# Norm steps beside context attention: which engine normalizes, which one stores the transposes, and in which slot they run

## The chip, the cores and the metric

The kernel runs on one core of a Trainium2 chip. The metric is the device time of one execution in microseconds. The core has five engines that run side by side and meet at semaphores: TensorE (PE in the profile), VectorE (DVE), ScalarE (ACT), GpSimd (POOL) and SyncE (SP), which issues nearly all DMAs.

## The reference

One transformer block over x of shape 2 x 1024 x 256, with a context of 2 x 154 x 192, 16 heads of 64, all in float32:

```python
h = layernorm(x, ln1);  x = attention(h, h,    sa_*) + x
h = layernorm(x, ln2);  x = attention(h, cond, ca_*) + x
h = layernorm(x, ln3);  p = h @ ff_w1 + ff_b1
a, gate = p[..., :1024], p[..., 1024:]
out = (a * gelu(gate)) @ ff_w2 + ff_b2 + x
```

`layernorm` is over the 256 features with gain and shift; `attention` projects queries, keys and values to 1024 columns, takes a softmax of the scaled scores and projects the result back to 256.

## The kernel before, in words

The order of all work is written out by hand in one loop after another (`tc.manual_schedule()`); no planner moves anything. Each engine does its instructions in the order in which the program issues them.

**Stages.** The two batches have eight head pairs each, so there are 16 units (`units`, eight of batch 0, then eight of batch 1). Self-attention comes first, 8 slots a unit (to about 725 us). Context attention follows with 48 slots, three a unit: slot c belongs to unit ui = c // 3 and n = c % 3, where n says which query tiles (3, 3 or 2 of 8) are scored. The gated layer comes last with 64 slots k, eight for each of eight blocks of two token tiles.

**One slot of context attention.** `cross_first(c)` (from L750) puts the scores of slot c into one of two PSUM tiles "s" (`sc`, L760) and takes the negated maxima on VectorE (`neg`, L765). ScalarE then takes the exponents (`p`, L776) with row sums; one slot later VectorE inverts the sums (`rden`, L784) and GpSimd scales (L787); two slots later VectorE transposes 32 x 32 blocks into `pT_ca` (L803), which DMAs regroup (L820). In this text exponents(c) and sc(c) are those of slot c. Beside it the slots carry other work:

- at n = 0, `cross_queries` of the next unit: `pq_ca` on TensorE (L353), copied to `q_ca` by ScalarE (L368);
- at n = 1, `cross_keys` of the next unit: `pk_ca` (L704), copied to `k_ca` by ScalarE (L708); in even units `context_values`, `pv_ca` (L720), copied to `v_ca` by ScalarE (L729, L730); and `cross_weigh`, the weighted sums `poc` (L839) of the unit two back, copied to `o_ca` by VectorE (L852);
- output projections `py_ca` or `py_sa` (`out_piece`, L457), whose results VectorE adds to x (L464).

A function that issues matmuls returns the store that empties its PSUM tile; `run` puts it on a list, `stores` or `adds`, and `flush` issues that list later.

**PSUM tiles.** There are three pools of two: "s" for scores and for the gated layer's `pa`; "mm" (`mm_tile`); "po" (`sum_tile`). At n = 1, `poc` takes both "po" tiles for its first half and both "mm" tiles for its second half, so it has to wait until whatever held them last has been read out.

**A norm beside other work.** `norm_beside(kind, b)` cuts a norm into steps and puts them on the list `side`. For the wide form (`narrow` is false: the third norm, "ff", and batch 1's second, "ca") a step takes two tiles: `stats` (VectorE, L231, L232), `deviation` (GpSimd, L237, L241), `normalize` (off, L247, then two instructions x to `xn`, L258 on GpSimd or L261 on ScalarE), and `turn`: four PE transposes (`ph`, L271) into one PSUM bank. The store of a turn applies gain and shift on the way from the bank to `hT` (L282 on VectorE, L286 on ScalarE): four pieces of 128 x 128 for "ca", two of 128 x 256 for "ff". `run_work(n, n_side, bank, n_sum)` takes at most `n_side` steps from `side`; a step that turns needs a bank, either `bank` or one of the n "mm" tiles, and otherwise stays where it is:

```python
needs_bank, needs, fn = side[0]
if needs_bank and not bank and n <= 0 or not added.issuperset(needs):
    break
```

So the arguments at each call of `run_work` in the slot loop say in which slots turns may run. The same function takes output projections from `outs`.

**Where the norms lie.** Batch 1's second norm runs in slots 6 to 15, batch 0's third norm in slots 36 to 45, batch 1's third norm in the gated layer from k = 8.

**The gated layer.** `gate_slot(k)` does eight matmuls `pa` (L921), the gelu on ScalarE (L927) and u on VectorE (L930). `sum_slot` does the two matmuls `pf` of the oldest u in `gated` (L944). From k = 5 on, up to two are taken a slot, and one u is always left. The first slots still finish context attention: `poc` of the last two units at k = 1 and k = 4, and the last output projections.

The lines of the profile before are in this listing:

Of the kernel before, what the change touches and what calls it, by code (L numbers as in the profile page):

```python
# [18 lines left out]
def tile_transformer_block(ctx: ExitStack, tc: tile.TileContext, a: dict, out: bass.AP):  # L19
# [4 lines left out]
    B, S, D = x.shape  # L24
# [5 lines left out]
    HP = NPAIR // 2  # L30
    NT = S // P
# [20 lines left out]
    TF = 2  # L52
# [42 lines left out]
    for n in names:  # L95
        k = n_of[n]
# [8 lines left out]
    for n in names[:2]:  # L105
        for r0 in range(0, P, HR):
            (nc.scalar if n == names[0] else nc.sync).dma_start(
                out=cols[r0:r0 + HR, row_of[n]:row_of[n] + NH],
# [95 lines left out]

    hT, vs, qk, oT = {}, {}, {}, {}

    spare = {"bank": mm_tile, "out": mm_tile}
    added = set()


# [1 line left out]
    def norm_pieces(kind, b, first=False):  # L212

        ln = {"sa": "ln1", "ca": "ln2", "ff": "ln3"}[kind]
        g0, b0 = row_of[ln + "_g"], row_of[ln + "_b"]
        st = {}  # L220
        nh = NC if kind == "ff" else NH
        order = tile_order(kind)

        def stats(t):
            if t == 0:
                st["hT"] = hT[kind, b] = p2.tile(
                    [P, nh, NC * S // nh], F32, tag="hT", name=f"hT_{ln}_{b}")
            if t % 2 == 0:
                st["mv", t] = small.tile([P, 2, 2], F32, tag="mv", name=f"mv_{ln}_{b}_{t}")
            s6 = small.tile([P, 6], F32, tag="st", name=f"st_{ln}_{b}_{t}")  # L230
            nc.vector.bn_stats(s6, xt[b, order[t] // GT][:, order[t] % GT, :])  # L231
            nc.vector.bn_aggr(st["mv", t // 2 * 2][:, t % 2, :], s6)  # L232

        def deviation(t):
            mv = st["mv", t]
            var = small.tile([P, 2], F32, tag="var", name=f"var_{ln}_{b}_{t}")
            (nc.vector if first else nc.gpsimd).tensor_scalar(  # L237
                var, mv[:, :, 1], EPS, 1.0, op0=ALU.add, op1=ALU.mult
            )
            rstd = small.tile([P, 2], F32, tag="rstd", name=f"rstd_{ln}_{b}_{t}")  # L240
            nc.gpsimd.tensor_tensor(rstd, var, power, ALU.pow)  # L241
            st["rstd", t] = rstd

        def normalize(t):
            rstd = st["rstd", t]
            off = small.tile([P, 2], F32, tag="off", name=f"off_{ln}_{b}_{t}")
            nc.vector.scalar_tensor_tensor(  # L247
                off, st["mv", t][:, :, 0], -1.0, rstd, op0=ALU.mult, op1=ALU.mult
            )
            pool, tag = (one, "xn") if narrow(kind, b) and not first else (pp_, "P")  # L250

            xn = pool.tile([P, nh, 2, D // nh], F32, tag=tag, name=f"xn_{ln}_{b}_{t}")
            st["xn", t] = xn
            for i in range(2):
                xs = xt[b, order[t + i] // GT][:, order[t + i] % GT, :]
                xs, own = xs.rearrange("p (c d) -> p c d", c=nh), xn[:, :, i, :]
                if kind == "ca" and not narrow(kind, b) or first and i == 1:
                    nc.gpsimd.tensor_scalar(  # L258
                        own, xs, rstd[:, i:i + 1], off[:, i:i + 1], op0=ALU.mult, op1=ALU.add)
                else:  # L260
                    nc.scalar.activation(  # L261
                        own, xs, AF.Identity, bias=off[:, i:i + 1], scale=rstd[:, i:i + 1])

        def turn(t):

            n = 2 if first else 1
            bank = mm_tile if first and t == 2 else spare["bank"]
            ph = [bank(f"ph_{ln}_{b}_{t}_{i}") for i in range(n)]
            for i in range(2 * D // P):

                nc.tensor.transpose(  # L271
                    ph[i * n * P // (2 * D)][:, i % (2 * D // P // n) * P:][:, :P],
                    st["xn", t].rearrange("p c i d -> p (c i d)")[:, i * P:(i + 1) * P], ident)

            def store():
                k = NC * 2 * P // nh
                for c in range(nh):
                    own = st["hT"][:, c, t // 2 * k:(t // 2 + 1) * k]
                    turned = ph[c * n // nh][:, c % (nh // n) * k:][:, :k]
                    gain, shift = cols[:, g0 + c:g0 + c + 1], cols[:, b0 + c:b0 + c + 1]  # L280
                    if first and c < nh // 2:
                        nc.vector.tensor_scalar(  # L282
                            own, turned, gain, shift, op0=ALU.mult, op1=ALU.add
                        )
                    else:
                        nc.scalar.activation(own, turned, AF.Identity, bias=shift, scale=gain)  # L286

            return store

        return (  # L290
            [lambda t=t: stats(t) for t in range(NT)],
            *([lambda t=t, f=f: f(t) for t in range(0, NT, 2)] for f in (deviation, normalize, turn)),
        )

# [6 lines left out]
    def narrow(kind, b):  # L301

        return kind == "sa" or kind == "ca" and b < B - 1
# [233 lines left out]
    stores, adds = [], []  # L537
    later = []

    def run(piece):  # L540
        done = piece()
        if done is not None:
            (adds if getattr(done, "adds", False) else stores).append(done)

    def flush(queue):
        for fn in queue:
            fn()
        queue.clear()
# [22 lines left out]
    def out_pieces(kind, b, half, tiles):  # L571
        outs.extend(lambda t=t: out_piece(kind, b, half, t) for t in tiles)
# [117 lines left out]
    CG = [(t, min(TG, NT - t)) for t in range(0, NT, TG)]  # L690
# [9 lines left out]
    def cross_keys(b, pr, bank=mm_tile):  # L700
        k = qk["ca", b, pr, "k"] = p2.tile([P, S], F32, tag="KT", name=f"k_ca{b}_{pr}")
        pk = bank(f"pk_ca{b}_{pr}")
        for c in range(2):
            nc.tensor.matmul(  # L704
                pk[:, :T], lhsT=wsl["ca", pr, "k"][:, c, :],
                rhs=ctxT[:, c, b * TP:b * TP + T], start=(c == 0), stop=(c == 1),
            )
        return lambda: nc.scalar.copy(k[:, :T], pk[:, :T])  # L708
# [160 lines left out]
    def cross_drain(c):  # L869

        n = c - 2
        if 0 <= n < CA:
            cross_turn(n)
# [11 lines left out]
    FF = B * NBL * NF  # L885
    gated, sums = [], {}
# [79 lines left out]
    with tc.manual_schedule():  # L966
# [85 lines left out]
        for c in range(CA):  # L1052
# [14 lines left out]
            ui, n = divmod(c, len(CG))  # L1067
            nxt = units[ui + 1] if ui + 1 < NU else None
# [9 lines left out]
                run(lambda: cross_keys(*nxt))  # L1078
            flush(adds)
            then = cross_first(c)  # L1080
            flush(stores)
            if c == 1:
                turn_groups(SA - 2)
            if n == 1 and ui > 1 and nxt:
                run(lambda: cross_keys(*nxt, sum_tile))
                flush(stores)
            flush(drain)
            flush(lates)
            lates.append(then())
# [5 lines left out]
            if c == 1:  # L1095
                run(lambda: cross_queries(*nxt))
            elif c == 2:
                run(lambda: cross_queries(*units[2], bank=sum_tile))
            elif c == 3:
                run(lambda: self_values(2 * NU - 1, 0))  # L1100
            elif c == 4:
                run(lambda: self_values(2 * NU - 1, 1))
                run(lambda: cross_keys(*nxt, sum_tile))
            elif n == 0 and ui:
                if nxt:
                    run(lambda: cross_queries(*nxt))
                run_work(0, 1, sum_tile)
            elif n == 1:

                run_work(0, 1, n_sum=1)  # L1110
                if ui % 2 == 0:
                    run(lambda: context_values(*units[ui]))
                run_work(1, 0)
                flush(adds)
                flush(stores)
                cross_weigh(c)
            elif n == 2:
                run_work(0, 1, sum_tile)
                if len(outs) > 2:
                    run_work(2, 0)  # L1120
            cross_regroup(c)
            for _ in range(min(2, len(later))):
                later.pop(0)()

        for k in range(FF):
            c = CA + k
            flush(adds)
            gate_slot(k)
            flush(stores)
            flush(lates)  # L1130
            if k == 3 * len(CG) - 1:
                norm_beside("ff", B - 1)
            cross_drain(c)
            cross_weigh(c)
            cross_regroup(c)
            if k == 0:
                out_pieces("ca", B - 1, 0, range(NT - 2 * TF, NT))
            if k == len(CG) + 1:
                out_pieces("ca", B - 1, 1, range(NT))
            if k > len(CG) + 1:  # L1140
                for _ in range(min(2, len(gated) - 1)):
                    run(sum_slot)
                flush(stores)
            run_work(2, 1)
            if later:
                later.pop(0)()
# [35 lines left out]
```

## Time and profile before

| what | value |
|---|---|
| median of 3 runs | 1145.99 us (1143.33 to 1146.7) |
| profiled execution, its own time | 1144.58 us |
| its span, first to last instruction | 1142.8 us |
| mean granted TensorE clock | 0.997 |
| busy: TensorE, VectorE, ScalarE, GpSimd | 1112.5, 835.4, 647.0, 672.7 us |
| context attention, about | 725 to 943 us |
| gated layer, about | 943 to 1140 us |

How to read the profile. A line of a stage table gives the stage, its length, and the busy time of PE, PEld (weight loads), DVE, ACT and POOL with their instruction counts, then the granted TensorE clock, the DMA share and GB/s. A line of the waits gives who waited for whom, the sum in microseconds, how many times, and the longest. A line of a timeline gives start, length, engine, source line, operation, output and inputs, shapes, count, and in brackets the idle time of the engine before it and what ended it. A line of the instructions of one source line gives the shortest, median and longest duration in ns, and the first and last start in us. A timeline's lengths overlap a little for pipelined matmuls, so the distance between two starts is what a piece takes.

### The profile page before, as it was taken

The page shows a single profiled execution, that of the slowest core. Times are in us where ns is not written, and L with a number is a line of the kernel's source. Part 1 is how long each engine was busy: PE and PEld are TensorE (multiplying, and loading weights), DVE is VectorE, ACT ScalarE, POOL GpSimd, SP SyncE. Part 2 cuts the span into 40 slices and gives each one's busy share as a digit, 9 for nine tenths or more (in the row PEclk, how much of TensorE's full clock was granted, in tenths as well). Part 3 has the DMA queues.
Part 4 walks back from the last instruction along what each step waited for, and adds up shares of the span by engine and source line. Part 5 has one row for each costly group of instructions (what it writes and reads, how often), then busy time and mean ns, then how long its engine had stood idle before and what let it go on. Part 6 is the DMA issues. An engine that isn't in the chain of part 4 may idle for free.

```text
span 1142.8 us, 36749 instructions
## 1 busy us (share of the span) xinstructions
PE 1112.5 (97%) x14372; PEld 688.5 (60%) x14372; DVE 835.4 (73%) x1183; ACT 647.0 (57%) x2082; POOL 672.7 (59%) x1568
## 2 busy tenths in 40 slices
PE   8999999999999999999999999998999989999998
PEld 5444444545545545545545554675777667888887
DVE  4888898898898999899988989766666754322222
ACT  4666666666765665666666666657555661041111
POOL 2777777878777777777777777756544542020000
PEclk9999999999999999999999999999999999999999
DMA  3212122201111111111111010256655523000000
GB/s 84 63 50 49 37 49 52 53 18 40 35 28 40 31 31 45 31 31 40 31 31 40 22 31 15 56 148 175 162 130 127 124 52 70 10 10 10 19 10 19
DMA packets 104910, 59.94 MB, mean 52 GB/s; under 512 B 32090, under 2 KB 95522, under 8 KB 104738
## 3 DMA queue, kind: packets, MB, share of 16 engines
q1 hardware_dynamic: 103506, 56.93, 20.9%
q8 instruction: 114, 1.87, 0.7%
q10 hardware_dynamic: 1232, 0.66, 0.2%
q14 instruction: 58, 0.48, 0.1%
HBM read 27.91 MB, written 2.10 MB: 26 GB/s over the span
## 4 chain that ended last, share of the span: by engine, by line
PE 85%; ACT 5%; DVE 3%; DMA 2%; POOL 2%; SPq 1%; issue 1%; DVEq 0%; POOLq 0%; ACTq 0%
PE po L526 18%; PE s L479 18%; PE pa L921 10%; PE py_sa L457 5%; PE py_ca L457 5%; PE pf L944 5%; PE pk_sa L353 4%; PE pq_sa L353 4%; PE pv_sa L384 4%; PE poc L839 4%; PE pq_ca L353 3%; ACT p L490 2%; PE sc L760 2%; SPq L500 1%; DVE st L641 1%
## 5 line engine op out<-in xcount | busy, mean ns | idle before, releaser
L490 ACT ACTIVATE p<-s,st 128x512 f32<-128x512 f32 x512 | 344.8, 686 | 204.9 <-DVE st L641 198.2
L591 POOL TENSOR_SCALAR p<-p,rd,ee 128x512 f32<-128x512 f32 x512 | 385.6, 767 | 45.6 <-DVE rd L587 44.3
L641 DVE TENSOR_REDUCE st<-s 128x2 f32<-128x1024 f32 x256 | 301.2, 1217 | 34.5 <-PE s L479 18.5
L605 DVE STREAM_TRANSPOSE pT<-p 128x1024 f32<-128x1024 f32 x256 | 302.2, 1217 | 0.3 <-POOL p L591 0.3
L479 PE MATMUL s<-k_sa,q_sa 64*32 64x512 f32 x4096 | 253.1, 596 | 13.0 <-ACT p L490 12.4
L526 PE MATMUL po<-pT,v_sa 64*64 64x256 f32 x4096 | 236.6, 380 | 0.8 <-DVE pT L605 0.8
L526 PEld LDWEIGHTS po<-pT,v_sa 64*64 64x64 f32 x4096 | 150.7, 133 | 110.7 <-issue 33.4
L787 POOL TENSOR_SCALAR p<-p,rden 128x154 f32<-128x154 f32 x256 | 96.8, 398 | 95.4 <-DVE rden L784 94.9
L479 PEld LDWEIGHTS s<-k_sa,q_sa 64*32 64x32 f32 x4096 | 65.9, 106 | 135.9 <-issue 66.0
L776 ACT ACTIVATE p<-sc,neg 128x154 f32<-128x154 f32 x256 | 96.6, 415 | 79.9 <-DVE rden L784 78.5
L930 DVE SCALAR_TENSOR_TENSOR u<-pa,cols,gate 128x256 f32<-128x256 f32 x64 | 31.0, 484 | 123.1 <-ACT gate L927 123.1
L921 PE MATMUL pa<-hT_ln,wf 128*128 128x256 f32 x512 | 120.7, 379 | 0.0
L927 ACT ACTIVATE gate<-pa,cols 128x256 f32<-128x256 f32 x64 | 30.3, 473 | 148.8 <-PE pa L921 148.7
L921 PEld LDWEIGHTS pa<-hT_ln,wf 128*128 128x128 f32 x512 | 96.9, 190 | 13.1 <-issue 0.2
L490 ACT ACTIVATION_READ_ACCUMULATOR p<-s,st 128x1 f32 x512 | 103.8, 203 | 0.0
L384 PEld LDWEIGHTS pv_sa<-sa_wv,hT_ln 64*128 64x128 f32 x1024 | 59.1, 188 | 17.4 <-DMA st<-st 7.5
L944 PE MATMUL pf<-wf,u 128*128 128x256 f32 x256 | 65.1, 379 | 0.2 <-DVE u L930 0.2
L514 POOL TENSOR_TENSOR zz<-ee,st 128x8 f32<-128x8 f32 x128 | 25.9, 202 | 66.4 <-ACT ee L512 66.4
L457 PE MATMUL py_ca<-ca_wo,o_ca 128*128 128x256 f32 x256 | 60.7, 388 | 4.3 <-ACT hT_ln L286 3.2
L384 PE MATMUL pv_sa<-sa_wv,hT_ln 64*128 64x128 f32 x1024 | 63.0, 276 | 0.6 <-ACT v_sa L393 0.6
L765 DVE TENSOR_REDUCE neg<-sc 128x6 f32<-128x924 f32 (+1 forms) x48 | 48.0, 1002 | 17.5 <-PE sc L760 17.4
L457 PE MATMUL py_sa<-sa_wo,o_sa 128*128 128x256 f32 x256 | 59.5, 385 | 0.0
(87 smaller groups left out, 1248.5 us busy)
## 6 DMA issues: line engine op xcount, KB each, us to landing
wf<-pT_ca SPq DMA_DIRECT2D x128, 128.0 KB, 2.5
st<-st SPq DMA_DIRECT2D x512, 1.0 KB, 1.8
v_sa<-v_sa SPq DMA_DIRECT2D x32, 256.0 KB, 3.4
sa_wq<-in_L_xattn_sa_wq_dram SPq DMA_DIRECT2D x32, 128.0 KB, 2.9
sa_wk<-in_L_xattn_sa_wk_dram SPq DMA_DIRECT2D x32, 128.0 KB, 2.9
sa_wv<-in_L_xattn_sa_wv_dram SPq DMA_DIRECT2D x32, 128.0 KB, 2.9
ca_wq<-in_L_xattn_ca_wq_dram SPq DMA_DIRECT2D x32, 128.0 KB, 3.0
wf<-in_L_xattn_ff_w_dram SPq DMA_DIRECT2D x12, 256.0 KB, 3.8
```

The costliest lines, as they stand in the source:

```text
L353: nc.tensor.matmul(pq[r][f:f + m, at:at + n], lhsT=wt[own, c, f:f + m], rhs=h[own, c, t0:t0 + n], start=(c == 0), stop=(c == NH - 1), tile ...
L384: nc.tensor.matmul(pv[r][:, i * P:(i + 1) * P], lhsT=h[own, c, i * P:(i + 1) * P], rhs=wt[own, c, :], start=(c == 0), stop=(c == NH - 1), ...
L457: nc.tensor.matmul(py[:, :D], lhsT=o[:, i, t * P:(t + 1) * P], rhs=wo[kind][:, half * HP + i, :], start=(i == 0), stop=(i == HP - 1),)
L479: nc.tensor.matmul(sc[a4 * KB:(a4 + 1) * KB, j, :], lhsT=q[r, c:c + KB], rhs=k[r, h * HB:(h + 1) * HB], start=True, stop=True, tile_positi ...
L490: nc.scalar.activation(pr[:, j, :], sc[:, j, :], AF.Exp, bias=st[:, 0, 0, i, j:j + 1], accum_out=st[:, 0, 1, i, j:j + 1],)
L526: nc.tensor.matmul(po[a2][j * DH:(j + 1) * DH, :QH // 2], lhsT=v[r, t, e, j * DH:(j + 1) * DH], rhs=pT[r, j * NK + n, :], start=(t == 0 an ...
L591: nc.gpsimd.tensor_scalar(pr[:, j, :], pr[:, j, :], rd[:, c:c + 1], ee[:, 0, c:c + 1], op0=ALU.mult, op1=ALU.mult,)
L605: nc.vector.transpose(halves[h][:, :, c:c + KB], groups.pop(0).rearrange("p j (n k) -> p (j n) k", k=KB))
L641: nc.vector.tensor_reduce(st[:, 0, 0, i, :], sc[i], AX.X, ALU.max, negate=True)
L787: nc.gpsimd.tensor_scalar(pr_[:, j, i, :T], pr_[:, j, i, :T], rden[:, j, i:i + 1], 1.0, op0=ALU.mult, op1=ALU.mult,)
L921: nc.tensor.matmul(pa[:, half, :TF * P], lhsT=w1[:, c, half * DF + f * P:half * DF + (f + 1) * P], rhs=h[:, c, t0 * P:(t0 + TF) * P], star ...
L944: nc.tensor.matmul(sums[blk][i][:, :D], lhsT=sums[blk, "u"][:, f, i * P:(i + 1) * P], rhs=w2[:, f, :], start=(f == 0), stop=(f == NF - 1),)
```

## The change

It is one diff with seven parts.

1. `normalize`: the condition for GpSimd no longer asks for "ca", so every wide norm is normalized by GpSimd; before, the third norm was normalized by ScalarE (16 instructions of 128 x 256).
2. A flag `spare["turned"]`: from slot 7 to the end of context attention it is set, and the stores of turns go to VectorE (16 pieces of 128 x 128 and 4 of 128 x 256); at the start of the gated layer it is cleared.
3. At n = 1, `cross_keys` is issued before the stores are flushed, and its copy is put at the head of the list, ahead of the query copies.
4. Turning steps may run at n = 1 with a "po" tile, their store issued at once, ahead of the output projections and `poc`; no longer at n = 0, and at n = 2 only in unit 3. So the turns of batch 1's second norm move from slots 11, 12, 14 and 15 to 11, 13, 16 and 19, and those of batch 0's third norm from 41, 42, 44 and 45 to 43, 46 and, in the gated layer, k = 0 and k = 1.
5. At the start of the gated layer, the list of output projections is filled before the drain, two projections run ahead of `poc` at k = 1, and the last eight projections are made available at k = 5 rather than k = 4, so after the `poc` of k = 4 the next `pa` follows.
6. Batch 1's third norm begins one slot later, at k = 9.
7. In the last two slots two u instead of one are left in `gated`.

```diff
-                if kind == "ca" and not narrow(kind, b) or first and i == 1:
+                if not narrow(kind, b) or first and i == 1:
                     nc.gpsimd.tensor_scalar(
...
-                    if first and c < nh // 2:
+                    if spare["turned"] or first and c < nh // 2:
                         nc.vector.tensor_scalar(
...
             then = cross_first(c)
+            if n == 1 and ui > 1 and nxt:
+                run(lambda: cross_keys(*nxt, sum_tile))
+                stores.insert(0, stores.pop())
             flush(stores)
             if c == 1:
                 turn_groups(SA - 2)
-            if n == 1 and ui > 1 and nxt:
-                run(lambda: cross_keys(*nxt, sum_tile))
-                flush(stores)
...
                 if nxt:
                     run(lambda: cross_queries(*nxt))
+                run_work(0, 1)
+            elif n == 1:
+
+                spare["turned"] = True
                 run_work(0, 1, sum_tile)
-            elif n == 1:
-
-                run_work(0, 1, n_sum=1)
+                flush(stores)
+                run_work(0, 0, n_sum=1)
                 if ui % 2 == 0:
                     run(lambda: context_values(*units[ui]))
                 run_work(1, 0)
...
             elif n == 2:
-                run_work(0, 1, sum_tile)
+                run_work(0, 1, sum_tile if ui == HP - 1 else None)
...
+        spare["turned"] = False
         for k in range(FF):
...
-            if k == 3 * len(CG) - 1:
+            if k == 3 * len(CG):
                 norm_beside("ff", B - 1)
+            if k == 0:
+                out_pieces("ca", B - 1, 0, range(NT - 2 * TF, NT))
+            if k == 1:
+                run_work(2, 0)
+                flush(adds)
             cross_drain(c)
             cross_weigh(c)
             cross_regroup(c)
-            if k == 0:
-                out_pieces("ca", B - 1, 0, range(NT - 2 * TF, NT))
-            if k == len(CG) + 1:
+            if k == len(CG) + 2:
                 out_pieces("ca", B - 1, 1, range(NT))
             if k > len(CG) + 1:
-                for _ in range(min(2, len(gated) - 1)):
+
+                for _ in range(min(2, len(gated) - (1 if k < FF - 2 else 2))):
                     run(sum_slot)
```

More of the change, by code (lines that the diff above doesn't have):

```diff
@@ L205, in tile_transformer_block @@
     hT, vs, qk, oT = {}, {}, {}, {}
-    spare = {"bank": mm_tile, "out": mm_tile}
+    spare = {"bank": mm_tile, "out": mm_tile, "turned": False}
     added = set()
```

## The prediction

> **What bounds the kernel now.** I read the page's first part, then the stage table, then TensorE's waits, then the timelines of the stalled stretches. TensorE is busy nearly all the time, so only its idle time can be won:
>
> ```profile
> PE 1112.5 (97%) x14372; PEld 688.5 (60%) x14372; DVE 835.4 (73%) x1183; ACT 647.0 (57%) x2082; POOL 672.7 (59%) x1568
> 770.00:802.00 32.00, 29.13 (x296) 19.02 (x295) 20.75 (x47) 21.02 (x90) 20.68 (x54) 1.00 0.69 172
> 802.00:909.00 107.00, 107.00 (x936) 76.82 (x938) 71.43 (x158) 64.11 (x294) 57.13 (x164) 1.00 0.56 131
> 909.00:931.00 22.00, 18.77 (x149) 12.88 (x141) 11.01 (x27) 12.16 (x46) 8.06 (x23) 0.92 0.29 62
> ```
>
> The second column is TensorE. The stage table shows where context attention leaves it idle: at 770 to 802, where batch 1's second norm runs beside it (slots 11 to 16 of 48), and after 909, where batch 0's third norm does (slots 41 to 45). Between them nothing is idle. The waits of TensorE in 770 to 966 are six rows:
>
> ```profile
> PE py_ca L457 <- ACT hT_ln L286: 3.2, 1, 3.2
> PE ph_ln L271 <- ACT xn_ln L261: 1.7, 2, 1.5
> PE poc L839 <- ACT hT_ln L286: 1.3, 1, 1.3
> PE poc L839 <- ACT v_ca L730: 1.0, 1, 1.0
> PE py_ca L457 <- DVE o_ca L852: 1.0, 2, 0.5
> PE ph_ln L271 <- POOL xn_ln L258: 0.6, 1, 0.6
> ```
>
> Together 8.8 us, four of the six rows due to ScalarE or its norm work. TensorE's timeline of the longest, and ScalarE's beside it:
>
> ```profile
> 916.67 0.79 PE L704 MATMUL pk_ca<-ctxT,ca_wk 96*128 96x154 f32 x4
> 920.68 3.44 PE L457 MATMUL py_ca<-ca_wo,o_ca 128*128 128x256 f32 x8 [3.23 <-ACT hT_ln L286]
> 923.97 1.89 PE L720 MATMUL pv_ca<-ca_wv,ctxT 96*128 96x256 f32 x8
> ```
>
> ```profile
> 917.64 1.11 ACT L261 ACTIVATE xn_ln<-x,off_ln,rstd_ln 128x256 f32<-128x256 f32 x2
> 918.62 1.10 ACT L368 ACTIVATE q_ca<-pq_ca 128x512 f32<-128x512 f32 x2
> 919.58 1.05 ACT L286 ACTIVATE hT_ln<-ph_ln,cols 128x256 f32<-128x256 f32 x2
> ```
>
> ScalarE runs six exponents, a normalization, two query copies, and only then the store that frees the PSUM bank for py_ca. That row also costs twice: its eight matmuls hold TensorE from 920.68 to 923.97, 3.29 us, where eight usually take 1.73 (the later py_ca in this slot).
>
> [...] after 3.23 us idle the granted clock of the stage is 0.92, and 3.29 - 1.73 = 1.56 us go. [...] six of these twelve ran at 770 to 802 beside a VectorE busy 20.75 of 32 us, and none takes over 557 ns:
>
> ```profile
> L258 POOL TENSOR_SCALAR xn_ln<-x,rstd_ln,off_ln x12: 547/549/557, 6.8 to 792.8; 128x256 f32<-128x256 f32 x12
> L282 DVE TENSOR_SCALAR hT_ln<-ph_ln,cols x8: 399/402/410, 8.2 to 15.1; 128x128 f32<-128x128 f32 x8
> ```
>
> **The change part by part.** TensorE's 14372 matmuls stay the same; only their order moves, and SP's list of DMAs is unchanged. I lay the new order on the old durations from start to start: ph .59 us, pk .63, sc .73 to .99, pq 3.53, py and pv 1.73, poc 2.75.
>
> (1) *Slots 41 to 43.* The two ph of slots 41 and 42 go; one comes after pk of slot 43. xn is on GpSimd (2 x .55 = 1.1 us) and issued slots earlier. ScalarE then does exponents(42) by about 915.7, the k copy when pk ends (916.3, +.35), q copies to 917.7. py_ca takes k's bank at 916.8: no wait. VectorE's queue in slot 43 is neg 1.1, rden .2, turns .9, four statistics 1.1, off .3, then the store; two pieces of 128x256, which I price at .42 to .48 each by L852 and L930 (no such store is in the trace): done at 920.0. poc needs that bank at 921.8. Slack 1.8. Gain: the hole (917.39 to 920.68) 3.29 + cold clock 1.56 + a ph that leaves .58 = **5.4**.
>
> (2) *Slots 44 to 47.* Without the ph between them, sc(44), sc(45), sc(46) follow each other, and sc(46) needs the score bank of sc(44), free when exponents(44) end. Before, that was 931.06 to 933.59, 2.53 us after sc(44) ended; so sc(46) waits 1.67. This takes the place of the 1.56 that the late xn cost; queued behind it on TensorE are ph, two py and poc. Then ph, py, py, and poc needs VectorE's store and py's add, behind neg 1.1, rden, turns .9: about .65 more. Row by row: before 12.22 us, after 11.86. Gain **.4**, where a ph that goes later is already .58.
>
> (3) *Start of the gated layer.* The two deferred ph come here, +1.2; ScalarE stores them behind the gates (py of k=1 needs that bank: free 19.6 us after sc(44) starts, needed at 19.7, so no room). Of the two .51 waits for o_ca, each .58 with its restart, the first stays, now in front of ph; the second goes, as pa follows poc where py did. Net **-.4** (loss).
>
> (4) *Slots 12 to 19 of batch 1's norm.* Slot 13: ph follows pk, hole .63 gone, but pv waits .5 for a query copy that is now behind the k copy. The next two poc banks wait for VectorE's four stores, 4 x .33 = 1.35 (two start .33 apart: 0.73 for the pair), behind neg, rden, turns, off: 1.05. The v_ca wait (really 1.67 from start to start) goes, ScalarE having shed 1.5 us of stores. Gain .7. Slot 16: poc is wanted 7.45 us after sc(14) starts, the store ends at 10.0, wait 2.55 against 1.44 + .16 now, with one ph less: loss .4. Slot 19 takes a ph without a wait: loss .6. Net **-.2**. Here the unknown is large: each store's end is a sum of six VectorE steps; bounds -2 and +1.5. Behind each store on VectorE stand the v_ca memset, the adds of py and the o_ca copies; who waits is poc.
>
> (5) *k copy before the query copies, 13 units.* In unit 10 (slot 31), pk ends 834.63; k is done at 835.0, the first query at 835.5; pv wants its bank at 836.20. Cover .7; taken at nothing. If gone, .34 a unit, 4.4 us.
>
> (6) *Last sums.* One pf pair moves behind the last pa, so the last u is covered: the .22 us hole goes. Gain **.2**.
>
> (7) *Batch 1's third norm*, one slot later, on GpSimd: 8 x .55 = 4.4 us in slots of 2.6 us where GpSimd is nearly free; TensorE does not wait there now and hT is not needed until k = 32. ff_b adds slip from slots 46 to 48 to after k = 1 (8 x .73 = 5.8 us, needed near k = 11). Nothing; if that cover failed, .5 to 1 us. GpSimd's eight xn beside attention fall into its idle gaps (4.4 us at 911).
>
> Sum: 5.4 + .4 - .4 - .2 + .2 = **5.4 us** off the profiled execution's 1144.58 (span 1142.8): 1139.2. The runs' median, 1145.99, is 1.4 above that execution; less 5.4 it gives 1140.6. I take 1140.0.
>
> **Rivals.**
> - *Given back* (chance .2): the bank of ph is now released at the end of VectorE's queue, and slots 13, 16 and 46 trade a ScalarE wait for a VectorE one about 1 us longer each than I reckon, and k=1 shows 1 us. Speaks for it: VectorE is already the busiest after TensorE (73%), and in slot 16 I find a longer wait myself. Against: slot 43 keeps 1.8 us of slack. Gain 5.4 - 4 = 1.4: 1144.
> - *Slower* (.09): ScalarE's queue now stops at the k copy until pk is done, the query copies behind it, and TensorE's next bank with them, in all 13 units. It decides when the first query copy comes over .7 us later than reckoned; at 1.4 us late each unit loses .7, 9.1 us in all, less 5.4: 3.7 slower, about 1149. Against it: exponents end before pk in units 9 to 13 anyway, so the copy waits only some .2 us.
> - *Larger gain* (.09): the stores are not last, slots 13 and 16 lose nothing: their 3.6 us of waits come back, 1136.5.
> - *My forecast* (.62): 1138 to 1142.5.
>
> **How the numbers follow.** About 0.3%, 3.4 us, is what a measurement of this kernel can tell from no change; faster by that means below 1142.55. The forecast lies under it almost wholly (.61), the larger gain wholly (.09), the first rival in a sixth (.03): faster .73. Within: .01 + .16, .17 with rounding. Slower: .09 and .01 of the first rival: .10. Range: 1136 to 1145, which leaves out the slow rival and part of the large gain.
>
> **What would show it.** Right: in slot 43 no py_ca wait on hT_ln, and a granted clock of 1.0 there; sc waiting some 1.7 us on exponents in slot 46; poc waiting on VectorE in slots 13 and 16; the last pf without a gap; one o_ca wait left. Wrong: py_ca or pv_ca waiting on query copies in unit after unit; a wait above 3 us with slow matmuls behind it; TensorE's idle sum in 770 to 966 not falling by 4 us.

## The result, and the profile after

The changed kernel takes 1138.26 us (median of 7 runs, 1136.75 to 1140.36) against 1144.66 us for the kernel before on the same chip (7 runs, 1142.03 to 1146.7): ratio 0.9946, 95% interval 0.9929 to 0.9962, which is 4.4 to 8.1 us. Predicted were 1140.0 us and a gain of 5.4 us. The profiled execution took 1138.26 us, its span 1136.5 us against 1142.8.

The first part of the page, then the table of stages after (both read as before: the second column of the table is TensorE, the eighth the granted clock):

```profile
PE 1109.5 (98%) x14372; PEld 689.9 (61%) x14372; DVE 841.2 (74%) x1203; ACT 632.0 (56%) x2046; POOL 681.2 (60%) x1584
```

```profile
770.00:802.00 32.00, 29.40 (x288) 19.19 (x282) 26.37 (x63) 17.69 (x83) 22.06 (x59) 1.00 0.77 190
802.00:909.00 107.00, 106.93 (x957) 77.05 (x955) 71.32 (x160) 61.59 (x284) 55.68 (x159) 1.00 0.55 129
909.00:931.00 22.00, 20.20 (x155) 15.07 (x152) 17.49 (x41) 14.61 (x70) 13.96 (x40) 0.92 0.42 92
```

ScalarE lost 15.0 us of work; GpSimd gained 8.5 and VectorE 5.8. TensorE's matmuls are the same 14372. The last row still has a clock of 0.92. The stall of slot 43 has gone, but in its place there is another piece at half clock, which is to say a stretch in which the granted TensorE clock is 0.5. TensorE's waits from 770 to 966, all the rows:

```profile
PE poc L839 <- DVE hT_ln L282: 1.9, 2, 1.7
PE sc L760 <- ACT p L776: 1.8, 1, 1.8
PE py_ca L457 <- DVE x L464: 0.8, 1, 0.8
PE ph_ln L271 <- DVE o_ca L852: 0.6, 1, 0.6
PE pv_ca L720 <- ACT q_ca L368: 0.5, 1, 0.5
```

8.8 us of waits have become 5.6, and the 3.2 us wait of py_ca on hT_ln is not among them. TensorE's timeline shows slot 43 without a hole; before, the same py_ca came 3.23 us late:

```profile
913.24 0.79 PE L704 MATMUL pk_ca<-ctxT,ca_wk 96*128 96x154 f32 x4
913.87 0.60 PE L271 MATMUL ph_ln<-ident,xn_ln 128*128 128x128 f32 x4
914.41 1.99 PE L457 MATMUL py_ca<-ca_wo,o_ca 128*128 128x256 f32 x8
916.24 1.89 PE L720 MATMUL pv_ca<-ca_wv,ctxT 96*128 96x256 f32 x8
```

Slots 45 and 46 of the same execution:

```profile
925.92 1.06 PE L760 MATMUL sc<-k_ca,q_ca 64*128 64x154 f32 x12 [1.80 <-ACT p L776]
926.90 0.98 PE L271 MATMUL ph_ln<-ident,xn_ln 128*128 128x128 f32 x4
927.67 5.02 PE L457 MATMUL py_ca<-ca_wo,o_ca 128*128 128x256 f32 x16
```

The predicted wait of sc on the exponents is there (1.80 us). The sixteen py_ca behind it take 5.02 us, where sixteen take 3.62 elsewhere. The granted clock is 0.5 from 927.1 to 930.5 us, and nothing in the prediction had that.

**Where the time went.** From here on the traces are compared in stretches, from the first score matmul of one slot to that of another ("k = 9": the first `pa` of that slot). The last column is what the prediction's sum gives for the stretch, minus for a gain.

| stretch | before | after | difference | predicted |
|---|---|---|---|---|
| start to slot 12 | 774.58 | 773.15 | -1.43 | 0 |
| slot 12 to 14 | 13.49 | 12.51 | -.98 | -.7 |
| slot 14 to 17 | 12.28 | 12.01 | -.27 | +.4 |
| slot 17 to 21 | 15.74 | 16.36 | +.62 | +.6 |
| slot 21 to 41 | 93.27 | 93.48 | +.21 | 0 |
| slot 41 to 44 | 20.91 | 15.03 | -5.88 | -5.4 |
| slot 44 to 47 | 12.22 | 12.84 | +.62 | -.4 |
| slot 47 to k = 9 | 51.06 | 52.45 | +1.39 | +.4 |
| k = 9 to the end | 149.21 | 148.65 | -.56 | -.2 |

The first row is no part of the change: from slot 7 to slot 12 both take 27.4 us, up to slot 7 the order is the same, and over the thirteen profiled kernels of this study the row runs from 772.1 to 776.1. Part of that scatter is the clock: before has a piece at half clock there, from 94.2 to 97.6 us, and after has none. The work around it takes 22.0 us in before and 19.9 to 20.6 in the ten traces without such a piece, which by itself is as much as the row's difference. Without the row the profiled difference is 4.85 us. The slow py_ca of slot 46 cost 1.43 us and do not come with every execution of the changed kernel (experiment 6); without that too it is 6.28 us.

### The profile page after: what moved, and what is told of

Read it like the earlier page. It is cut to its first block, busy times and chain, and to the rows that moved or that the text cites. A ratio compares the mean times of both kernels' runs of the same rounds, so it can differ in the third digit from the quotient of the medians.

```text
span 1136.5 us, 36749 instructions
## 1 busy us (share of the span) xinstructions
PE 1109.5 (98%) x14372; PEld 689.9 (61%) x14372; DVE 841.2 (74%) x1203; ACT 632.0 (56%) x2046; POOL 681.2 (60%) x1584
## 4 chain that ended last, share of the span: by engine, by line
PE 79%; ACT 6%; DVE 4%; DMA 4%; POOL 3%; SPq 2%; issue 2%; DVEq 0%; POOLq 0%; ACTq 0%
PE po L526 16%; PE s L479 16%; PE pa L921 9%; PE py_sa L457 5%; PE pf L944 5%; PE py_ca L457 5%; ACT p L490 4%; PE pk_sa L353 4%; PE pq_ca L353 4%; PE pv_sa L384 4%; PE poc L839 4%; PE pq_sa L353 3%; PE sc L760 2%; SPq L500 2%; DVE st L641 2%; DMA st<-st 2%
```

## The experiments

All runs are against the kernel before on the same chip; its medians were 1145.31, 1144.99 and 1145.19 us in the three groups. "After" is the changed kernel. A stretch that no edit touches comes out the same within .2 us from run to run, unless a piece of it runs at half clock; only start to slot 12 and slot 17 to 21 scatter.

**1. GpSimd's normalization alone**, in the kernel before:

```diff
-                if kind == "ca" and not narrow(kind, b) or first and i == 1:
+                if not narrow(kind, b) or first and i == 1:
```

> The kernel before with one edit: the third norm is normalized by GpSimd; stores, slots and copies stay. Theory (order of ScalarE's queue): in slot 43 the py_ca wait shrinks only by the two normalizations that stood ahead of the store, 3.2 to about 2.1 us, and the wait of ph for xn in slot 45 (1.7 us) turns into a short wait of sc for exponents; 2 to 4 us faster than before, the larger end if the clock stays up after the shorter wait. Rival (ScalarE's load alone was the cause): the py_ca wait is gone and nearly the whole gain of the change is there, 5 to 6 us.

Measured: 1143.27 us, ratio 0.9975 (0.9965 to 0.9985). Slots 41 to 44 take 17.63 us, 3.28 less than before, but slots 44 to 47 take 14.72, 2.50 more. Its waits:

```profile
PE ph_ln L271 <- POOL xn_ln L258: 3.2, 3, 2.4
PE py_ca L457 <- ACT hT_ln L286: 0.9, 1, 0.9
```

Of the 3.2 us wait of py_ca .9 are left, since ScalarE still stores the turn. And in the old slots GpSimd's xn comes too late for its turn: ph waits 2.4 us in slot 45, with half clock behind it from 930.8 to 934.2 us. Of the 2.50 us about .9 is the longer wait (2.4 us in place of 1.5) and the rest the clock. So neither expectation was quite right: the whole gain, about 2 us, is at the low end of the theory's, but the py_ca wait shrank further than to 2.1 us, and what the normalization gains in one slot it gives back in good part two slots on.

**2. The stores back on ScalarE**, the rest as after:

```diff
-                spare["turned"] = True
                 run_work(0, 1, sum_tile)
```

> The changed kernel with the stores of turns left on ScalarE (the flag is never set); GpSimd normalization and new slots stay. Theory (the store's engine decides, because in the new slots ScalarE's store stands behind the six exponents of its slot): poc waits about 2.5 us in slot 13, 3.5 to 5 us in slot 16 with a half-speed clock behind it, about 1.4 us in slot 46; 4 to 7 us slower than the changed kernel, so near the kernel before. Rival (only the slots count): the same time as the changed kernel within 1 us.

Measured: 1144.4 us, ratio 0.9992 (0.9985 to 0.9999). Slot 43 is as good as after (15.03 us from 41 to 44). What is lost is lost in slots 12 to 14 (13.83 us, +1.32) and 14 to 17 (16.80, +4.79), and .8 us in slot 46, if after's slow piece there is left out:

```profile
PE poc L839 <- ACT hT_ln L286: 5.9, 3, 4.0
```

```profile
794.96 0.65 PE L839 MATMUL poc<-wf,v_ca 64*64 64x256 f32 x4
799.56 1.54 PE L839 MATMUL poc<-wf,v_ca 64*64 64x256 f32 x10 [3.95 <-ACT hT_ln L286]
```

Once the turn stands right ahead of poc, its store on ScalarE lies behind six exponents, and poc waits 3.95 us in slot 16 against 1.73 with VectorE. The rest of the 4.79 us, some 2.6, is half clock from 798.0 to 804.8 us. The theory holds. So the stores on VectorE are the price at which the later turn is to be had; in slot 43 itself they are worth nothing.

**3. The turns in their old slots**, normalization and stores as after:

```diff
-                run_work(0, 1)
+                run_work(0, 1, sum_tile)
             elif n == 1:
                 spare["turned"] = True
-                run_work(0, 1, sum_tile)
-                flush(stores)
-                run_work(0, 0, n_sum=1)
+                run_work(0, 1, n_sum=1)
...
-                run_work(0, 1, sum_tile if ui == HP - 1 else None)
+                run_work(0, 1, sum_tile)
```

> The changed kernel with turns back in their old slots (11, 12, 14, 15; 41, 42, 44, 45), stores on VectorE and all normalizations on GpSimd. Theory (the bank's release decides, not the slot): slot 43 waits at most 1 us, ph again stands between the scores of slots 44 to 46 so their wait for exponents is mostly filled and the clock stays up; equal to the changed kernel or 1 to 3 us faster. Rival (the new slots carry the gain): the py_ca wait in slot 43 is back near 3 us, 4 to 5 us slower than the changed kernel.

Measured: 1141.41 us, ratio 0.9956 (0.9943 to 0.997). Slots 41 to 47 take 31.86 us in place of 27.87, and 47 to k = 9 49.89 in place of 52.45, as two turns fewer are left for it. Summed from slot 12 it is 1.96 us worse than after. Its largest wait is GpSimd's xn again (3.4 us, longest 2.4), not the store. Both expectations missed: the old slots are slower, but by 2 us in the traces and not by 4 to 5, and slot 43 has no py_ca wait over .4 us. Both traces have one piece at half clock in slots 44 to 47, so it does not make the difference.

**4. The normalization back on ScalarE**, turns and stores as after (the condition of experiment 1, reversed).

> The changed kernel with the third norm's normalization back on ScalarE (16 instructions of 128x256), the rest as changed. Theory (once the turns are moved to slots 43, 46, k = 0 and k = 1, ScalarE has gaps of 3.8 and 5.0 us where these instructions fall, so the engine matters little): 1138.5 to 1139.5, slots 41 to 44 15.0 to 15.6 us. Rival (GpSimd's normalization is itself what the gain in slot 43 comes from): slots 41 to 44 above 17 us with a py_ca wait on ScalarE, and over 1140.5. The normalization on GpSimd with the old slots gained 3.3 us there, of 5.9, so that run leaves both open.

Measured: 1137.46 us, ratio 0.995 (0.9933 to 0.9967). Slots 41 to 44 15.03 us, as after; 44 to 47 11.41; only 47 to k = 9 is .33 longer. Slots 14 to 17, whose program is that of after, took 13.69 in place of 12.01; the 1.68 us are half clock (below). The rival falls: with the turns moved, GpSimd's normalization is worth some .4 us.

**5. The k copy behind the query copies again:**

```diff
                 run(lambda: cross_keys(*nxt, sum_tile))
-                stores.insert(0, stores.pop())
```

> The changed kernel with one line out: the copy of k_ca is flushed in its old place, behind the query copies. My theory (part 5 of the prediction: the copy order is worth nothing either way, because .7 us cover the query copies): 1138.3 us, within 0.7 of the changed kernel; only in slot 13 does the .55 us wait of pv_ca on the query copy go, and in slot 43 pk_ca's bank comes .55 us a copy later, which costs under 1 us. Rival 1 (the k copy ahead delays the query copies in unit after unit): the stretch from slot 21 to slot 41, 93.48 us in the changed kernel, becomes shorter by over 1 us. Rival 2 (the k copy ahead is what the new order of slot 43 lives on, since py_ca takes k's bank): slots 41 to 44 grow from 15.03 us by 1.1 us or more, with a wait of py_ca on k_ca, and the run is near 1140.

Measured: 1138.65 us, ratio 0.9955 (0.9943 to 0.9967). Slots 21 to 41 93.31 us against 93.48: the copies' order costs the quiet units at most .17 us in all. Slots 41 to 44 take 15.65 us, .62 more:

```profile
PE py_ca L457 <- ACT k_ca L708: 1.2, 2, 0.6
```

So the rival that the prediction priced at 9 us is wrong, and "nothing" is nearly right: where a turn and a py_ca follow pk, the copy ahead saves .6 us. Of rival 2 the mechanism is right and its 1.1 us too much. (Slots 14 to 17 took 13.70 us here, with poc at half clock behind waits of .6 and 1.1 us.)

**6. The last sums as before, in the changed kernel; and 7. the last sums alone, in the kernel before** (there the lines of the diff change places):

```diff
-                for _ in range(min(2, len(gated) - (1 if k < FF - 2 else 2))):
+                for _ in range(min(2, len(gated) - 1)):
```

> The changed kernel with the end of the gated layer as before: one u is left in the last slots, not two. My theory (part 6): only the last u is uncovered again, a .2 us gap ahead of the last pf, so from k = 9 to the end 148.9 us in place of 148.65, and about 1138.5. Rival (the measured .5 us of that stretch all come from here): 149.15 us. Second rival (the stretch's gain comes from batch 1's third norm, one slot later and on GpSimd, not from the sums): 148.65, no change.

> The kernel before with part 7 of the change alone: two u are left in the last two slots. Theory (the .5 us from k = 9 to the end is this part, since undoing it in the changed kernel gave all of it back): 149.21 - .5 = 148.7 us from k = 9 to the end, 1144.5 us in all. Rival (it needs the later third norm as well): 149.2. The run also shows a second time the context slots of the kernel before. If the half clock after a wait of 3.23 us in slot 43 follows from the wait, slots 41 to 44 take 20.9 us again with eight py_ca in 3.3 us; if it is chance there too, as after the 1.7 to 1.8 us waits (slow in two of the executions, fast in three others of the same program part), they may take 19.3.

Measured: experiment 6 149.14 us from k = 9 to the end (+.49), experiment 7 148.72 (-.49). So this part is worth .49 us with either kernel, as the first rival had it and not the .2 of my theory, and the third norm on GpSimd one slot later at most .07. The end of the kernel before shows the gap:

```profile
1137.10 1.03 PE L944 MATMUL pf<-wf,u 128*128 128x256 f32 x4
1138.35 1.13 PE L944 MATMUL pf<-wf,u 128*128 128x256 f32 x4 [0.22 <-DVE u L930]
```

The times of whole runs can't show so little: 1138.7 us, ratio 0.9948 (0.9933 to 0.9962), and 1145.79 us, ratio 1.0004 (0.9996 to 1.0013).

Both executions bear on the slow py_ca too. Experiment 6 has the same wait in slot 46, word for word, and then sixteen matmuls at full clock:

```profile
926.25 1.06 PE L760 MATMUL sc<-k_ca,q_ca 64*128 64x154 f32 x12 [1.80 <-ACT p L776]
927.24 0.66 PE L271 MATMUL ph_ln<-ident,xn_ln 128*128 128x128 f32 x4
927.73 3.62 PE L457 MATMUL py_ca<-ca_wo,o_ca 128*128 128x256 f32 x16
```

It takes 11.41 us from slot 44 to 47 where after took 12.84. Experiment 4 shows the reverse in slot 16, where after had no slow matmul behind the same wait:

```profile
795.79 0.86 PE L839 MATMUL poc<-wf,v_ca 64*64 64x256 f32 x10 [1.72 <-DVE hT_ln L282]
...
797.13 1.90 PE L839 MATMUL poc<-wf,v_ca 64*64 64x256 f32 x12
```

The second twelve take 1.02 us in the execution of after. Over the profiled executions with the same program there: after the 1.8 us wait of slot 46 one of five has half clock (after; not experiments 2, 4, 5, 6), after the 1.72 us wait of slot 16 one of seven (experiment 4). In slot 45 of the old order, after 1.50 + .16 us, one of two: 44 to 47 takes 13.81 us in experiment 7 and 12.22 in the kernel before. After the 3.23 us wait of slot 43 both profiled executions have it (20.91 and 21.14 us), and so has the one after 3.95 us (experiment 2). But even the 3.23 us wait is not followed by half clock every time: of the 72 executions of the kernel before in the three groups, five, all on one chip, have a mean granted clock of 1.000, and a single piece of 3.41 us at half clock would bring it to 0.9985. The last section lays out where such pieces begin.

**8. Work put into slot 45.** The sc of slot 46 waits 1.80 us for exponents; output projections are at hand to fill it. Two in one kernel, one in the next:

```diff
                 run_work(0, 1)
+                if ui == NU - 1:
+                    run_work(2, 0)      # the second kernel: run_work(1, 0)
```

> The changed kernel with the two output projections of slot 46 issued in slot 45, between the scores of slots 45 and 46. Theory (sc of slot 46 waits for the exponents of slot 44 because nothing stands between, and the pause is what halves the clock behind it): the wait of 1.8 us and the 1.4 us of slow py_ca go, 2.5 to 3.2 us faster than the changed kernel. Rival (the wait moves to poc of slot 46, which needs VectorE's store): the same time within 1 us, with a poc wait of about 2 us.

> The changed kernel with one output projection (eight matmuls, 1.73 us) taken in slot 45, ahead of the scores of slot 46, which there wait 1.80 us for the exponents of slot 44. With two projections the wait went but the weighted sums of slot 46 then stood 1.98 us behind VectorE's store. Theory A (VectorE's queue, max of slot 46 first and then the store, sets the end, and each projection ahead of the scores delays both equally): the score wait falls to about .1, the py_ca that ran at half clock after it is fast again, no wait over .5 us comes in its place, and slots 44 to 47 and the start of the gated layer together gain about 1.8 + 1.4 = 3.2 us less the .4 us that a new wait may take: from slot 44 to k = 9 some 62.3 us in place of 65.29. Theory B (whatever is filled in ahead comes back as a wait of poc on the store): 65 us, no gain. The wait and the slow clock are separate: if the wait goes and the slow matmuls stay, the clock was not lowered by the wait.

Measured: with two 1139.32 us, ratio 0.9937 (0.9923 to 0.995), slots 44 to 47 13.59 us with poc at half clock; with one 1136.06 us, ratio 0.9932 (0.9908 to 0.9955), 11.41 us. The wait of sc is gone in both, and poc waits in its place, 1.98 and 1.58 us. The profile names no releaser ("issue"), but VectorE's timeline beside it does, with one projection. TensorE's resumes at 930.38:

```profile
930.38 1.15 PE L839 MATMUL poc<-wf,v_ca 64*64 64x256 f32 x14 [1.58 <-issue]
```

```profile
927.29 1.10 DVE L765 TENSOR_REDUCE neg<-sc 128x6 f32<-128x924 f32 x1
928.31 0.18 DVE L784 RECIPROCAL rden<-den 128x6 f32<-128x6 f32 x1
928.41 0.86 DVE L803 STREAM_TRANSPOSE pT_ca<-p 128x320 f32<-128x320 f32 x2
929.20 0.17 DVE L247 SCALAR_TENSOR_TENSOR off_ln<-mv_ln,rstd_ln 128x2 f32<-128x2 f32 x1
929.29 0.98 DVE L282 TENSOR_SCALAR hT_ln<-ph_ln,cols 128x256 f32<-128x256 f32 x2
```

The store ends at 930.27, the poc follows. Theory B's mechanism holds: from slot 44 to 47 it is 11.41 us with and without the projection (experiment 6), where the clock held. From slot 44 to k = 9 that makes 63.86 us, after's 65.29 less its 1.43 us of half clock. Slot 46's store stands behind the reciprocal of slot 45's sums. In this execution VectorE has no idle time from 922.1 to 930.6 us, and slot 45's exponents end at 928.28, .03 us before the reciprocal starts, so its own queue and ScalarE hold the store about equally; in experiment 6, without the projection, the reciprocal waits .25 us for the exponents. The median is 2.2 us under after's all the same. All five executions of the kernel with one projection have a mean clock of 1.000, of after two of seven; how much of the 2.2 us that explains stays open.

**9. The first projection of k = 1 into a "po" tile**, with one projection in slot 45:

```diff
             if k == 1:
-                run_work(2, 0)
+                run_work(0, 0, n_sum=1)
+                run_work(1, 0)
                 flush(adds)
```

> The changed kernel with one projection in slot 45, ahead of the scores of slot 46, and at k = 1 the first of the two projections put into a 'po' tile. With the first edit alone slots 44 to 47 took 11.41 us, as without it where the clock held; the wait moved from sc to poc. Theory: py_ca at k = 1 waits .81 us for the 'mm' tile whose add stands on VectorE behind a transposition, while both 'po' tiles are free, so the wait goes and k = 47 to k = 9 takes 51.65 us in place of 52.45; slots 44 to 47 stay at 11.4; near 1135.5. Rival (the add of the 'po' projection then comes late for poc, which takes both 'po' tiles first): 52.4 us, with a poc wait of some .8 us at k = 1.

In after, the add on VectorE and the py_ca that waits for it:

```profile
942.33 0.41 DVE L464 TENSOR_TENSOR x<-py_ca,x 128x256 f32<-128x256 f32 x1
942.80 3.72 PE L457 MATMUL py_ca<-ca_wo,o_ca 128*128 128x256 f32 x16 [0.81 <-DVE x L464]
```

Measured: 1137.54 us, ratio 0.9933 (0.9921 to 0.9945); 47 to k = 9 51.37 us in place of 52.45. The .81 us wait of py_ca on x is gone, with 1.08 us, so the theory holds for the stretch. The expected 1135.5 us were missed: the ratio is that of the projection alone (0.9932), and start to slot 12 was 2.9 us longer in this profile than in that one.

**10. That, without the turn in slot 46:**

```diff
-                run_work(0, 1, sum_tile)
+                run_work(0, 1, sum_tile if ui < NU - 1 else None)
                 flush(stores)
```

> The last kernel without the turn in slot 46: batch 0's third norm turns in slot 43 and at k = 0, 1 and 2. In slot 46 the store of the turn stands on VectorE behind the reciprocal, which waits for the exponents of slot 45, so poc waits 1.58 us for its bank. Theory (the store is what poc waits for; what is left is the adds of the projections in the same queue): slots 44 to 47 take 10.0 to 10.6 us in place of 11.41, of which .5 us is the turn itself that comes back at k = 2; a net gain of .3 to .9 us over the kernel with the turn. Rival (the adds, behind the same reciprocal, release poc hardly sooner): 10.9 us, which is only the turn, and no net gain.

Measured: 1135.46 us, ratio 0.9914 (0.99 to 0.9928), the fastest kernel here, about 9.7 us under the kernel before. Slots 44 to 47 take 10.39 us, 1.02 less; 47 to k = 9 takes 51.81, .44 more for the turn. Net .58, as the theory had it. Against after, the stretches from slot 44 to k = 9 give 62.20 in place of 65.29 us, or 63.86 without the slow py_ca.

```profile
PE poc L839 <- DVE x L464: 0.7, 1, 0.7
PE ph_ln L271 <- DVE o_ca L852: 0.6, 1, 0.6
```

What is left in slot 46 is the add of a projection, in the same queue of VectorE.

## Why the prediction was right, and where its steps were off

The mechanism, the place and nearly the size were right. Point by point, with the half clock of slot 46, which does not come every time, taken out:

- **(1) Slots 41 to 43: 5.88 us, predicted 5.4.** The wait and the half clock went, as reckoned. Of the .5 us above the forecast .3 are in the scores: without a ph between them, sc of slots 41 and 42 and pq take 4.85 us in place of 5.15. The step counts the 1.56 us of half clock as certain, which it is not. The five executions of the kernel before at a mean clock of 1.000 have a median of 1140.99 us, the two of after 1137.19 and 1137.56. By these few the change is worth some 3.6 us where the clock stays up on both sides (the forecast without its half clock is 3.8), and half clock, which the kernel before meets more often, is at least a part of the rest of the 6.4 us (the mean of the 72 clocks is 0.9965, of after's seven 0.998, which is one such piece more in each execution). What the step did not say is which part carries it. Experiments 1 and 4 tell: the normalization alone gains 3.28 us there and gives 2.50 back, in part through the clock; with the later turn ScalarE's normalization does as well.
- **(2) Slots 44 to 47: .81 us gained (11.41), predicted .4.** The term mis-sized is poc's ".65 more" for VectorE's store: in experiment 6, with no slow py_ca, there is no such wait. The sc wait was 1.80 for a predicted 1.67. In the profiled execution the stretch lost .62 us instead, since the clock fell to 0.5 (927.1 to 930.5 us).
- **(3) Start of the gated layer: 1.39 us lost, predicted .4.** The terms that the step states, 1.2 less .58, already make .6. The step "so no room" looked at ScalarE's store, but the bank that py_ca at k = 1 lacks is that of the projection before it, whose add VectorE runs behind u, a reciprocal, two transpositions into pT and an off (L464 at 942.33 us). That is .81 us of wait, and experiment 9 has 1.08 us back by another tile; with .81 the step would have read -1.4.
- **(4) Slots 12 to 21: predicted a loss of .2 (its terms, .7 less .4 less .6, make .3); slots 12 to 17 gained 1.25.** Both poc waits were reckoned about .8 too long: 1.05 for a measured .22 in slot 13, 2.55 for 1.73 in slot 16. VectorE's six steps from neg to the end of the store take 3.37 us from start to end in slot 16, where their durations add to 3.7, since each starts about .1 us before the last one ends (1.00, then 2.04, 2.13, 2.92 and 3.01 to 4.37 us after sc of slot 16); the store's own 1.36 was as reckoned. That overlap is .3 of the .8; the prediction gives its ends as sums only, so where the rest lies stays open. Slots 17 to 21 lost .62 for a predicted .6, but that stretch ran from 15.65 to 16.83 us over kernels with the same program there (15.01 to 16.22 over three with the program of before), so its size stays open, and why it scatters too.
- **(5) k copy: nothing, predicted nothing** in the quiet units (.17 us); it is worth .62 in slot 43, inside (1).
- **(6) Last sums: .49 us, predicted .2.** The step took the gap, .22 us, as the whole cost. Start to start, the last two pf were 1.25 us apart where others are .86: here a gap of .22 cost .39, and a part of this I had allowed for in (3) and not here. The other .1 is the last four pf themselves, 1.13 us long for the usual 1.03.
- **(7) Batch 1's third norm: nothing** (at most .07 us), as predicted.

The sum, 5.4 against 6.28, came near in part by luck, because errors cancelled: (1), (2), (4) and (6) together gained 2.0 us more than reckoned, (3) lost 1.0 more, and slots 21 to 41 lost .2. Of the rivals, "Slower" fell with experiment 5. "Given back" was right in one place, k = 1. The larger gain was half right on poc: slot 13 lost almost nothing, slot 16 waited 1.73 us.

## What to carry to other kernels

A stall behind a late store has several remedies that are not additive: here moving the turn later needs the store on a short queue (poc waits 5.9 us on ScalarE's store, 1.9 on VectorE's) but hardly needs GpSimd's normalization (.55 us for 128 x 256 where ScalarE takes .60; worth some .4 us in experiment 4). When a hole is filled, ask what the next consumer's release hangs on: sc's 1.80 us in slot 46 came back as 1.58 or 1.98 us at poc, which hung on VectorE's queue and the next slot's exponents. Compare traces by stretches between fixed points, and look for half clock on both sides before a difference of 1.5 us is laid to the change.

## What the hardware showed that was not expected

Waits of 1.5 to 2 us were followed by 3.41 us at half clock in some executions and not in others of the same program. In slot 46 of after the py_ca started .427 us apart until 930.23 us, then .216; that cost 1.43 us. In slot 16 of experiment 4 it cost 1.68, in slot 45 of experiment 7 1.6. For a change worth 6 us that is a quarter of it, in a single profile.

In these traces a piece does not begin where a wait begins or ends. In before that of slot 43 begins at 920.25 us, .43 us before py_ca resumes (920.68); in after that of slot 46 begins at 927.09 us, 1.17 us after sc has resumed (925.92). Before 1130 us the half-clock pieces of the thirteen traces last 3.41 us each (3.413 in before and after), and in one place two follow each other (experiment 2, 798.0 to 804.8 us). Within a trace their starts lie whole multiples of that length apart: in before 94.22 and 920.25 us, 826.03 us or 242 lengths, in experiment 7 921.15 and 934.80 us, 13.65 us or 4. The pieces at the very end fit as well: in after 208.21 us behind the piece of slot 46 (1135.31 us), 61 lengths, in before 221.87 us behind that of slot 43 (1142.11 us), 65. Where in the span these points lie differs between executions: 921.15 us in experiment 7 is .90 us off the 920.25 us of before. Why the 1.80 us wait of slot 46 is followed by half clock in after and not in experiment 6 is not shown by this, and no run was made to test it.
